# Two graph layers on one core: where the operands of the second layer lie, and what TensorE does ahead of the last transposes of the first

## The chip, the cores and the metric

The kernel runs on one core of a Trainium2 chip. The metric is the device time of one execution in microseconds (us); the time of the kernel before is the median of 3 runs. Beside it there is one profiled execution with a trace of every engine. TensorE is PE in the profile (PEld is its load of weights), VectorE is DVE, ScalarE is ACT, GpSimd is POOL, and SyncE (SP) issues most of the DMAs.

## The reference

x is 2500 x 1024, there are 80,000 edges with a source, a destination (sorted, and denser at low numbers) and a weight. Cut to what matters:

```python
h = relu(layernorm(x))
x = x + segment_sum((h @ W0)[src] * edge_weight[:, None], dst)      # layer 1
h = relu(layernorm(x))
row, col = dst plus every node itself as destination, src plus every node itself as source
deg = number of edges in each row (the node itself counted)
dis = deg ** -0.5
x = x + segment_sum((dis[row] * dis[col])[:, None] * (h @ W1.T + b)[col], row)   # layer 2
```

In the second layer no edge has a weight of its own. So its sum is a product of a matrix of counts (2500 x 2500, how many edges run from one node to another, the node itself included) with the rows dis * (h @ W1.T + b), and dis once more on the outside.

## The kernel before

The nodes lie in 20 tiles of 128 rows (the last has 68). Layer 1 first makes `support` = h @ W0 for all tiles (L281). Then each tile of destinations is summed: the four thickest tiles (0 to 3) as products with dense weight matrices (`multiplied`, L588), the other 16 by gathers of 128 rows of `support` at a time (`gathered`, L564): POOL gathers a block into `msg` (8 buffers), DVE makes a one-hot matrix, ACT makes `hi` and DVE `lo`, two parts of the weighted rows for matmuls in a faster format, and PE adds four matmuls of them to `sums` (L581). When a tile's sums are complete, `finish` (L540) adds x (L543), normalizes (`normed`, DVE and ACT), transposes (`transposed`, L530: 8 transposes on PE, copied by ACT), multiplies with W1 (L554, 16 matmuls in plain fp32, two halves of 512 columns), adds the bias (L558) and stores the result in `hid_d[t]`. Along with this, `count_group` builds the matrix of counts tile by tile, `counts`, which is stored as `cnat` (L497) and summed into `total`.

Layer 2 begins at L667: `deg` is the sum over `total`, `dis` follows from it (L668 to L670). Then comes the flag `missing` (L671 to L681): it tells whether any edge found no place, by a matmul with ones (L676) and comparisons of its result; at the very end of the program a second, general way is taken if it is not zero. After `first.close()` (L682) the pools of layer 2 are opened. For every tile, in the order of `ORDER`, a row buffer (3 of them) is loaded from `hid_d[t]` (L691), ACT makes `hi` (L693) and DVE `lo` (L695): both stay in SBUF for the whole of layer 2, 8 KB in each partition for a tile. For each row of tiles `counts_of` loads the counts with a transposing DMA into `cT` (L701, two buffers) and ACT casts them to `bT` (L703, two buffers). 80 matmuls (L721: 20 tiles, hi and lo, two halves) make the sums of one row; rows 0 and 1 are made together, so that each operand tile serves 8 matmuls as soon as it is there. `row` (L706) adds x1 and stores.

What sets the order: every engine runs its own list of instructions in the order that a scheduler fixed when the program was built. The scheduler takes an instruction when its own estimate says that it is ready, and of those that are ready the one that stands first in the code; so work that stands late in the code can run early. `order_behind(i, other)` (L273) tells it that `i` must come after `other` on the same engine. The tiles and the counting of layer 1 are dealt out by a plan written by hand (L464 to L663).

What sets the places: SBUF pools are laid one after the other from the low end, those with `side="right"` from the high end, and a closed pool's bytes are given out again. With `reuse_waits="tile"` a tile waits only for the users of the bytes that it covers; without it, for all users of the pools beneath. The sizes in one partition, from the code: `keep` 2 KB, then `lay` (total, bias, src_p, row_p, wgt_p, base_i, low, key, wpart, iota16, in this order) about 30 KB, `work` 25, `ohs` 15.5, `cpool` 15.4, `wpool` (the 8 pieces of W1) 32.8, `dense` (4 matrices of 10.2) 41; from the right `gather` (msg 8 x 4.1, oh_r, hi, lo) 50.7. Layer 2 has `lay2` (20 tiles x 8.2 KB), which begins where `lay` began, and then `work2` (rows 3 x 4.1, cT 2 x 5.1, bT 2 x 10.2), 43 KB. [...]Before, one pool holds pT (2 banks), mm (2 x 2), cb (2), in the order of their first use; `psum2` of layer 2 lays three sums `mm2` of 2 banks each over the first six.

Of the kernel before, what the change touches and what calls it, by code (L numbers as in the profile page):

```python
# [9 lines left out]
F32 = mybir.dt.float32  # L10
F32R = mybir.dt.float32r
# [5 lines left out]
ALU = mybir.AluOpType  # L17
DVE = mybir.EngineType.DVE

P = 128  # L20
# [18 lines left out]

OPENING = 8  # L40
TAIL = 48

ORDER = (3, 4, 5, 6, 2, 7, 8, 9, 1, 10, 11, 12, 13, 0, 14, 15, 16, 17, 18, 19)

# [2 lines left out]
def direct(  # L47
# [26 lines left out]
    nc = tc.nc  # L74
# [14 lines left out]
    def rows(t):  # L89
        return min(P, N - t * P)  # L90
# [24 lines left out]


    first = ctx.enter_context(ExitStack())
    lay = first.enter_context(tc.tile_pool(name="lay", bufs=1))
    work = first.enter_context(tc.tile_pool(name="work", bufs=2))
    psum = first.enter_context(tc.tile_pool(name="psum", bufs=2, space=bass.MemoryType.PSUM))  # L120
    ohs = first.enter_context(tc.tile_pool(name="ohs", bufs=8))
    cpool = first.enter_context(tc.tile_pool(name="cpool", bufs=3))
    wpool = first.enter_context(tc.tile_pool(name="wpool", bufs=1, reuse_waits="tile"))
    sup_ctx = tc.tile_pool(name="sup", bufs=4, side="right")
    sup = sup_ctx.__enter__()
    prep_ctx = tc.tile_pool(name="prep", bufs=1)
# [158 lines left out]

    def products(t):
        hT, rstd = ready.pop(t)
        mm = psum.tile([P, 2, H], F32, name="mm")
        yield from product(hT, w0_sb, mm)
        row = sup.tile([P, D], F32, name="row", bufs=2)  # L290
        nc.scalar.activation(row, mm.rearrange("p h d -> p (h d)"), AF.Copy, scale=rstd)
        nc.sync.dma_start(support[t * P:t * P + rows(t), :], row[:rows(t), :])
# [123 lines left out]
    def count_group(t, g, a, b):  # L416
        nonlocal last_count

        w = WINDOWS[t][1]
        if t not in counts:  # L420
            counts[t] = cpool.tile([P, NT, P], F16, name="counts")
            nc.scalar.copy(counts[t].rearrange("p t w -> p (t w)"), zero.to_broadcast([P, NT * P]))
            nc.vector.tensor_copy(counts[t][:, t, :rows(t)], ident[:, :rows(t)])
            if t < DENSE:
                dense[t] = dpool.tile([P, NT, P], F32, name="dense")
                nc.scalar.copy(dense[t].rearrange("p t w -> p (t w)"), zero.to_broadcast([P, NT * P]))
        if g % 4 == 0:
            bases[t] = nc.values_load_multi_w_load_instructions(
                base_i[0:1, g:g + 4], engines=[DVE], min_val=0, max_val=P - w,
                skip_runtime_bounds_check_because="a row of a tile")[1]  # L430
        v = bases[t][g % 4]
        cb = psum.tile([P, 512], F32, name="cb")
        ab = []
        for k in range(a, b):
            oh_low = ohs.tile([P, P], BF, name="oh_low")
            nc.vector.tensor_scalar(oh_low, iota16[:, :P], low[:, k:k + 1], None, op0=ALU.is_equal)  # L436
            oh_key = ohs.tile([P, KW], BF, name="oh_key")
            nc.vector.tensor_scalar(oh_key[:, :NT * w], iota16[:, :NT * w], key[:, k:k + 1], None,  # L438
                                    op0=ALU.is_equal)
            last_count = nc.tensor.matmul(  # L440
                cb[:, :NT * w], oh_low, oh_key[:, :NT * w], start=(k == a), stop=(k == b - 1))
            if t < DENSE:
                wl = ohs.tile([P, 3, P], BF, name="wl")
                for i in range(3):
                    nc.scalar.activation(wl[:, i, :], oh_low, AF.Copy, scale=wpart[:, i, k:k + 1])  # L445
                ab.append((wl, oh_key))
        to = counts[t][:, :, ds(v, w)]
        nc.vector.tensor_tensor(to, cb[:, :NT * w].rearrange("p (t w) -> p t w", w=w), to, op=ALU.add)  # L448
        if t < DENSE:
            for j, (wl, oh_key) in enumerate(ab):  # L450
                for i in range(3):
                    last_count = nc.tensor.matmul(  # L452
                        cb[:, 256:256 + NT * w], wl[:, i, :], oh_key[:, :NT * w],
                                     start=(j == 0 and i == 0), stop=(j == len(ab) - 1 and i == 2))
            to = dense[t][:, :, ds(v, w)]
            nc.vector.tensor_tensor(to, cb[:, 256:256 + NT * w].rearrange("p (t w) -> p t w", w=w), to,
                                    op=ALU.add)
        if b == K0[t + 1]:
            nc.vector.tensor_tensor(total, counts[t], total, op=ALU.add)
            to_store.append([6, t])  # L460
# [66 lines left out]
    gpool = first.enter_context(tc.tile_pool(name="gather", bufs=2, side="right", reuse_waits="tile"))  # L527


    def transposed(v, into):  # L530
        for k0 in range(0, KC, 4):
            pT = psum.tile([P, 4, P], F32, name="pT")
            for k in range(4):
                nc.tensor.transpose(pT[:, k, :], v[:, (k0 + k) * P:(k0 + k + 1) * P], ident)  # L534
            nc.scalar.copy(into[:, k0:k0 + 4, :], pT)
            yield 0.7, 0.0, 0.6

# [85 lines left out]

    def steps_of(tiles):
        for t in tiles:
            sums = psum.tile([P, 2, H], F32, name="mm")
            n = NT if t < DENSE else TILE_BLOCKS[t]
            for j, took in enumerate((multiplied if t < DENSE else gathered)(t, sums)):
                if j == n - 1:
                    rest = finish(t, sums)  # L630
                    takes(*next(rest))
                    waiting.append(rest)
                yield took
# [34 lines left out]
    nc.vector.tensor_scalar(dis, deg, 1.0, None, op0=ALU.max)  # L668
    nc.scalar.activation(dis, dis, AF.Sqrt)
    nc.vector.reciprocal(dis, dis)  # L670
    nc.vector.tensor_reduce(placed[:, 1:2], deg, axis=mybir.AxisListType.X, op=ALU.add)  # L671
    over = lay.tile([P, NT], F32, name="over")
    nc.vector.tensor_scalar(over, deg, 2048.0, None, op0=ALU.is_gt)
    nc.vector.tensor_reduce(placed[:, 2:3], over, axis=mybir.AxisListType.X, op=ALU.add)
    ps = psum.tile([P, 4, P], F32, name="pT")
    nc.tensor.matmul(ps[:, 0, :3], ones, placed, start=True, stop=True)  # L676
    lost = lay.tile([1, 3], F32, name="lost")
    for i, n in enumerate((E, E + N, 0)):
        nc.vector.tensor_scalar(lost[:, i:i + 1], ps[0:1, 0, i:i + 1], float(n), None, op0=ALU.not_equal)
    nc.vector.tensor_add(lost[:, 0:1], lost[:, 0:1], lost[:, 1:2])  # L680
    nc.vector.tensor_add(missing, lost[:, 0:1], lost[:, 2:3])  # L681
    first.close()  # L682


    lay = ctx.enter_context(tc.tile_pool(name="lay2", bufs=1, reuse_waits="tile"))
    work = ctx.enter_context(tc.tile_pool(name="work2", bufs=2, reuse_waits="tile"))
    psum = ctx.enter_context(tc.tile_pool(name="psum2", bufs=2, space=bass.MemoryType.PSUM, reuse_waits="tile"))
    his, los = {}, {}
    for t in ORDER:
        hf = work.tile([P, D], F32, name="rows", bufs=3)  # L690
        nc.sync.dma_start(hf, hid_d[t])  # L691
        his[t] = lay.tile([P, D], F32R, name=f"hi{t}")
        nc.scalar.activation(his[t], hf, AF.Copy, scale=dis[:, t:t + 1])  # L693
        los[t] = lay.tile([P, D], F32R, name=f"lo{t}")
        nc.vector.scalar_tensor_tensor(los[t], hf, dis[:, t:t + 1], his[t].bitcast(F32),  # L695
                                       op0=ALU.mult, op1=ALU.subtract)

# [8 lines left out]
    def row(r, mm):  # L706
        xh = work.tile([P, D], F32, name="rows", bufs=3)
        nc.sync.dma_start(xh, x1_d[r])
        nc.vector.scalar_tensor_tensor(xh, mm.rearrange("p h d -> p (h d)"), dis[:, r:r + 1], xh,  # L709
                                       op0=ALU.mult, op1=ALU.add)  # L710
        nc.sync.dma_start(out[r * P:r * P + rows(r), :], xh[:rows(r), :])


    for rs in [(0, 1)] + [(r,) for r in range(2, NT)]:
        bTs = [counts_of(r) for r in rs]
        mms = [psum.tile([P, 2, H], F32, name="mm2", bufs=3) for r in rs]
        for k in ORDER:
            for bT, mm in zip(bTs, mms):
                for v in (his[k], los[k]):
                    for h in range(2):  # L720
                        nc.tensor.matmul(mm[:, h, :], bT[:rows(k), k, :], v[:rows(k), h * H:(h + 1) * H],  # L721
                                         start=(k == ORDER[0] and v is his[k]),
                                         stop=(k == ORDER[-1] and v is los[k]))
        for r, mm in zip(rs, mms):
            row(r, mm)


def kernel(tc, edges, xT, *args):
# [338 lines left out]
```

## Time and profile before

| what | us |
|---|---|
| median of 3 runs (1786.69 to 1789.98) | 1788.44 |
| the profiled execution | 1799.45 |
| its span, first to last instruction | 1797.5 |
| counting ends: last store of counts (L497) | 1124.4 |
| last dense matmul (L594) | 1286.1 |
| last `lo` of the gathers (L577) begins | 1385.5 |
| sums of the last tile added to x (L543) begin | 1390.1 |
| last tile's transposes (L534) begin | 1396.7 |
| first matmul of layer 2 (L721) begins | 1413.1 |
| rows 0 and 1 done, first output step (L709) begins | 1457.5 |
| last output step (L709) begins | 1789.0 |

A timeline line reads: start, duration, engine, line, operation, output <- inputs, shapes, count, and in brackets how long the engine was idle before it and what ended that. A line of the chain of work that ended last reads: start, duration, engine, output, line. In a table of windows each engine has its busy time and its number of instructions.

### The profile page before, as it was taken

How to read it: one execution, taken by the hardware profiler on the slowest of the kernel's cores; microseconds unless marked ns; L12 is line 12 of the kernel's file. 1: busy time of each engine (PE TensorE's matmuls, PEld its weight loads, DVE VectorE, ACT ScalarE, POOL GpSimd, SP SyncE). 2: the span in 40 equal slices, each digit the busy share in tenths (PEclk: the TensorE clock that was granted, in tenths of full speed). 3: DMA queues.
4: the chain of work that ended last, by engine and by line, in shares of the span. 5: the costliest groups of instructions: out<-in, count | busy, mean ns of one | idle time of the engine just before them, and what ended most of it. 6: DMA issues, size and time to landing. Idle time of an engine off the chain costs nothing. (4 is left out here: it accounts for less than half of the span.)

```text
span 1797.5 us, 21334 instructions
## 1 busy us (share of the span) xinstructions
PE 1674.1 (93%) x6506; PEld 1036.6 (58%) x6506; DVE 1207.7 (67%) x3051; ACT 903.0 (50%) x1476; POOL 479.4 (27%) x457
## 2 busy tenths in 40 slices
PE   6999999999788897988999998999899999999998
PEld 2465555544354554544556554655566568888886
DVE  5788888898698796888899897877787330000000
ACT  3499999961165454455456443555565431111110
POOL 3000000000066453555545544555463000000000
PEclk9999999999899998999999999999999999999999
DMA  8413121132799896898889888988986874342420
GB/s 274 171 37 97 51 77 60 39 83 71 242 350 355 281 314 235 281 342 259 300 307 329 307 268 278 344 321 320 320 298 212 229 196 108 77 115 76 115 62 32
DMA packets 217329, 369.95 MB, mean 206 GB/s; under 512 B 115662, under 2 KB 135128, under 8 KB 217206
## 3 DMA queue, kind: packets, MB, share of 16 engines
q0 software_dynamic: 54832, 199.25, 31.5%
q1 hardware_dynamic: 162374, 169.25, 30.0%
q8 instruction: 53, 0.87, 0.2%
q14 instruction: 70, 0.57, 0.1%
HBM read 300.79 MB, written 54.56 MB: 198 GB/s over the span
## 5 line engine op out<-in xcount | busy, mean ns | idle before, releaser
L575 ACT ACTIVATE hi<-msg,wgt_p 128x1024 fp32r<-128x1024 f32 x378 | 426.1, 1147 | 375.9 <-PE mm L581 281.1
L569 POOL DMA_INDIRECT msg<-support,src_p x378 | 464.1, 1228 | 515.2 <-DVE lo L577 178.0
L577 DVE SCALAR_TENSOR_TENSOR lo<-msg,wgt_p,hi 128x1024 fp32r<-128x1024 f32 x378 | 478.7, 1281 | 94.9 <-ACT hi L575 54.2
L281 PE MATMUL mm<-w,hT 128*128 128x512 f32 x640 | 314.4, 603 | 2.4 <-ACT hT L173 2.4
L581 PE MATMUL mm<-hi,oh_r 128*128 128x512 f32 x756 | 291.0, 466 | 19.9 <-ACT hi L575 14.6
L554 PE MATMUL pT<-w,vT 128*128 128x512 f32 x640 | 303.1, 595 | 0.0
L581 PE MATMUL mm<-lo,oh_r 128*128 128x512 f32 x756 | 280.4, 451 | 16.9 <-DVE lo L577 16.0
L445 ACT ACTIVATE wl<-oh_low,wpart 128x128 bf16<-128x128 bf16 x891 | 262.0, 418 | 0.0
L721 PE MATMUL mm<-lo,bT 128*128 128x512 f32 (+1 forms) x800 | 248.1, 392 | 3.7 <-DVE lo L695 3.3
L721 PE MATMUL mm<-hi,bT 128*128 128x512 f32 (+1 forms) x800 | 247.6, 392 | 3.3 <-ACT bT L703 2.0
L709 DVE SCALAR_TENSOR_TENSOR rows<-mm,dis,rows 128x1024 f32<-128x1024 f32 x20 | 25.7, 1284 | 308.0 <-PE mm L721 307.3
L594 PE MATMUL mm<-msg,dense 128*128 128x512 f32 (+1 forms) x320 | 166.6, 636 | 38.9 <-DMA msg<-support 38.9
L581 PEld LDWEIGHTS mm<-hi,oh_r 128*128 128x128 f32 x756 | 141.7, 192 | 103.2 <-issue 46.4
L581 PEld LDWEIGHTS mm<-lo,oh_r 128*128 128x128 f32 x756 | 138.3, 192 | 102.8 <-DVE lo L577 49.5
L438 DVE TENSOR_SCALAR oh_key<-iota,key 128x200 bf16<-128x200 f16 (+12 forms) x675 | 195.5, 292 | 3.0 <-PE cb L452 2.8
L703 ACT CAST bT<-cT 128x2560 fp32r<-128x2560 f16 x20 | 46.6, 2335 | 261.3 <-PE mm L721 257.8
L554 PEld LDWEIGHTS pT<-w,vT 128*128 128x128 f32 x640 | 120.8, 190 | 94.5 <-issue 80.4
L721 PEld LDWEIGHTS mm<-lo,bT 128*128 128x128 f32 (+1 forms) x800 | 149.8, 188 | 40.0 <-DVE lo L695 8.9
L721 PEld LDWEIGHTS mm<-hi,bT 128*128 128x128 f32 (+1 forms) x800 | 150.3, 189 | 36.3 <-ACT bT L703 2.4
L448 DVE TENSOR_TENSOR counts<-cb,counts 128x200 f32 (+13 forms) x296 | 138.9, 470 | 47.6 <-PE cb L440 40.8
L436 DVE TENSOR_SCALAR oh_low<-iota,low 128x128 bf16<-128x128 f16 x675 | 168.3, 253 | 1.3 <-ACT wl L445 1.1
L281 PEld LDWEIGHTS mm<-w,hT 128*128 128x128 f32 x640 | 107.8, 192 | 62.9 <-issue 56.7
(141 smaller groups left out, 1144.4 us busy)
## 6 DMA issues: line engine op xcount, KB each, us to landing
msg<-support SPq DMA_DIRECT2D x76, 512.0 KB
xt<-in_x SPq DMA_DIRECT2D x38, 512.0 KB
cnat<-counts SPq DMA_DIRECT2D x20, 640.0 KB
x_d<-xt SPq DMA_DIRECT2D x20, 512.0 KB
hid_d<-hn SPq DMA_DIRECT2D x20, 512.0 KB
rows<-hid_d SPq DMA_DIRECT2D x20, 512.0 KB
rows<-x_d SPq DMA_DIRECT2D x20, 512.0 KB
hT<-in_xT SPq DMA_DIRECT2D x19, 512.0 KB
```

Of the source, the lines that this page charges most:

```text
L281: on_pe(nc.tensor.matmul(mm[:, h, :], vT[:, k, :], ws[k][:, h * H:(h + 1) * H], start=(k == 0), stop=(k == KC - 1)))
L436: nc.vector.tensor_scalar(oh_low, iota16[:, :P], low[:, k:k + 1], None, op0=ALU.is_equal)
L438: nc.vector.tensor_scalar(oh_key[:, :NT * w], iota16[:, :NT * w], key[:, k:k + 1], None, op0=ALU.is_equal)
L445: nc.scalar.activation(wl[:, i, :], oh_low, AF.Copy, scale=wpart[:, i, k:k + 1])
L448: nc.vector.tensor_tensor(to, cb[:, :NT * w].rearrange("p (t w) -> p t w", w=w), to, op=ALU.add)
L554: on_pe(nc.tensor.matmul(mm, vT[:, k, :], w1_sb[k][:, h * H:(h + 1) * H], start=(k == 0), stop=(k == KC - 1)))
L569: nc.gpsimd.indirect_dma_start(out=msg, out_offset=None, in_=support, in_offset=bass.IndirectOffsetOnAxis(ap=src_p[:, k:k + 1], axis=0))
L575: nc.scalar.activation(hi, msg, AF.Copy, scale=wgt_p[:, k:k + 1])
L577: nc.vector.scalar_tensor_tensor(lo, msg, wgt_p[:, k:k + 1], hi.bitcast(F32), op0=ALU.mult, op1=ALU.subtract)
L581: i = nc.tensor.matmul(sums[:, h, :], oh, v[:, h * H:(h + 1) * H], start=(j == 0 and v is hi), stop=(j == n - 1 and v is lo))
L594: i = nc.tensor.matmul(sums[:, h, :], dense[t][:rows(k), k, :], msg[:rows(k), h * H:(h + 1) * H], start=(k == 0), stop=(k == NT - 1))
L721: nc.tensor.matmul(mm[:, h, :], bT[:rows(k), k, :], v[:rows(k), h * H:(h + 1) * H], start=(k == ORDER[0] and v is his[k]), stop=(k == ORDE ...
```

## The change

The pools of layer 1 are laid in another order, and PSUM is split into three pools (cb, mm, pT). Layer 2's operands are in two pools: `late` for the last 11 tiles of ORDER, laid in reverse order from where `lay` began, then `work2`, then `early` for the first 9 tiles. The loads and splits stand inside the loop over the tiles of rows 0 and 1. The first of the last tile's 8 transposes (`turned[-KC]`) is put behind the 24th matmul of layer 2. The flag is computed after row 4, with a buffer of mm2 for its matmul.

```diff
+EARLY = 9
+BETWEEN = 3
...
-    lay = first.enter_context(tc.tile_pool(name="lay", bufs=1))
-    work = first.enter_context(tc.tile_pool(name="work", bufs=2))
+    lay = first.enter_context(tc.tile_pool(name="lay", bufs=1, reuse_waits="tile"))
+    work = first.enter_context(tc.tile_pool(name="work", bufs=2, reuse_waits="tile"))
+    psum_c = first.enter_context(tc.tile_pool(name="psum_c", bufs=2, space=bass.MemoryType.PSUM))
+    psum_m = first.enter_context(tc.tile_pool(name="psum_m", bufs=2, space=bass.MemoryType.PSUM))
     psum = first.enter_context(tc.tile_pool(name="psum", bufs=2, space=bass.MemoryType.PSUM))
-    ohs = first.enter_context(tc.tile_pool(name="ohs", bufs=8))
-    cpool = first.enter_context(tc.tile_pool(name="cpool", bufs=3))
     wpool = first.enter_context(tc.tile_pool(name="wpool", bufs=1, reuse_waits="tile"))
+    ohs = first.enter_context(tc.tile_pool(name="ohs", bufs=8, reuse_waits="tile"))
+    cpool = first.enter_context(tc.tile_pool(name="cpool", bufs=3, reuse_waits="tile"))
...
-        mm = psum.tile([P, 2, H], F32, name="mm")
+        mm = psum_m.tile([P, 2, H], F32, name="mm")
...
-        cb = psum.tile([P, 512], F32, name="cb")
+        cb = psum_c.tile([P, 512], F32, name="cb")
...
+    turned = []
+
     def transposed(v, into):
...
-                nc.tensor.transpose(pT[:, k, :], v[:, (k0 + k) * P:(k0 + k + 1) * P], ident)
+                turned.append(nc.tensor.transpose(pT[:, k, :], v[:, (k0 + k) * P:(k0 + k + 1) * P], ident))
...
-            sums = psum.tile([P, 2, H], F32, name="mm")
+            sums = psum_m.tile([P, 2, H], F32, name="mm")
...
-    nc.vector.tensor_reduce(placed[:, 1:2], deg, axis=mybir.AxisListType.X, op=ALU.add)
-    over = lay.tile([P, NT], F32, name="over")
...
-    nc.vector.tensor_add(missing, lost[:, 0:1], lost[:, 2:3])
     first.close()
-    lay = ctx.enter_context(tc.tile_pool(name="lay2", bufs=1, reuse_waits="tile"))
+    psum = ctx.enter_context(tc.tile_pool(name="psum2", bufs=2, space=bass.MemoryType.PSUM, reuse_waits="tile"))
+    late = ctx.enter_context(tc.tile_pool(name="late", bufs=1, reuse_waits="tile"))
+    his, los = {}, {}
+
+    def parts_of(t, pool):
+        his[t] = pool.tile([P, D], F32R, name=f"hi{t}")
+        los[t] = pool.tile([P, D], F32R, name=f"lo{t}")
+
+    for t in ORDER[:EARLY - 1:-1]:
+        parts_of(t, late)
     work = ctx.enter_context(tc.tile_pool(name="work2", bufs=2, reuse_waits="tile"))
-    psum = ctx.enter_context(tc.tile_pool(name="psum2", bufs=2, space=bass.MemoryType.PSUM, reuse_waits="tile"))
-    his, los = {}, {}
-    for t in ORDER:
+    early = ctx.enter_context(tc.tile_pool(name="early", bufs=1, reuse_waits="tile"))
+    for t in ORDER[:EARLY]:
+        parts_of(t, early)
+
+    def split(t):
         hf = work.tile([P, D], F32, name="rows", bufs=3)
         nc.sync.dma_start(hf, hid_d[t])
-        his[t] = lay.tile([P, D], F32R, name=f"hi{t}")
         nc.scalar.activation(his[t], hf, AF.Copy, scale=dis[:, t:t + 1])
-        los[t] = lay.tile([P, D], F32R, name=f"lo{t}")
         nc.vector.scalar_tensor_tensor(los[t], hf, dis[:, t:t + 1], his[t].bitcast(F32),
                                        op0=ALU.mult, op1=ALU.subtract)
...
+    def all_placed():
+        nc.vector.tensor_reduce(placed[:, 1:2], deg, axis=mybir.AxisListType.X, op=ALU.add)
+        over = keep.tile([P, NT], F32, name="over")
+        nc.vector.tensor_scalar(over, deg, 2048.0, None, op0=ALU.is_gt)
+        nc.vector.tensor_reduce(placed[:, 2:3], over, axis=mybir.AxisListType.X, op=ALU.add)
+        ps = psum.tile([P, 2, H], F32, name="mm2", bufs=3)
+        nc.tensor.matmul(ps[:, 0, :3], ones, placed, start=True, stop=True)
+        lost = keep.tile([1, 3], F32, name="lost")
+        for i, n in enumerate((E, E + N, 0)):
+            nc.vector.tensor_scalar(lost[:, i:i + 1], ps[0:1, 0, i:i + 1], float(n), None, op0=ALU.not_equal)
+        nc.vector.tensor_add(lost[:, 0:1], lost[:, 0:1], lost[:, 1:2])
+        nc.vector.tensor_add(missing, lost[:, 0:1], lost[:, 2:3])
...
     for rs in [(0, 1)] + [(r,) for r in range(2, NT)]:
         bTs = [counts_of(r) for r in rs]
         mms = [psum.tile([P, 2, H], F32, name="mm2", bufs=3) for r in rs]
         for k in ORDER:
+            if rs[0] == 0:
+                split(k)
             for bT, mm in zip(bTs, mms):
                 for v in (his[k], los[k]):
                     for h in range(2):
-                        nc.tensor.matmul(mm[:, h, :], bT[:rows(k), k, :], v[:rows(k), h * H:(h + 1) * H],
+                        i = nc.tensor.matmul(mm[:, h, :], bT[:rows(k), k, :], v[:rows(k), h * H:(h + 1) * H],
...
+            if rs[0] == 0 and k == ORDER[BETWEEN - 1]:
+                order_behind(turned[-KC], i)
         for r, mm in zip(rs, mms):
             row(r, mm)
+        if rs[0] == 4:
+            all_placed()
```

More of the change, by code (lines that the diff above doesn't have):

```diff
@@ L670, in direct @@
     nc.vector.reciprocal(dis, dis)
-    nc.vector.tensor_reduce(placed[:, 1:2], deg, axis=mybir.AxisListType.X, op=ALU.add)
-    over = lay.tile([P, NT], F32, name="over")
[L673 to L680, printed above, removed]
-    nc.vector.tensor_add(missing, lost[:, 0:1], lost[:, 2:3])
-    first.close()
-    lay = ctx.enter_context(tc.tile_pool(name="lay2", bufs=1, reuse_waits="tile"))
+    first.close()
+    psum = ctx.enter_context(tc.tile_pool(name="psum2", bufs=2, space=bass.MemoryType.PSUM, reuse_waits="tile"))
[6 more added lines that the diff above has]
+        parts_of(t, late)
     work = ctx.enter_context(tc.tile_pool(name="work2", bufs=2, reuse_waits="tile"))
-    psum = ctx.enter_context(tc.tile_pool(name="psum2", bufs=2, space=bass.MemoryType.PSUM, reuse_waits="tile"))
-    his, los = {}, {}
-    for t in ORDER:
+    early = ctx.enter_context(tc.tile_pool(name="early", bufs=1, reuse_waits="tile"))
+    for t in ORDER[:EARLY]:
+        parts_of(t, early)
+    def split(t):
         hf = work.tile([P, D], F32, name="rows", bufs=3)
         nc.sync.dma_start(hf, hid_d[t])
-        his[t] = lay.tile([P, D], F32R, name=f"hi{t}")
         nc.scalar.activation(his[t], hf, AF.Copy, scale=dis[:, t:t + 1])
-        los[t] = lay.tile([P, D], F32R, name=f"lo{t}")
         nc.vector.scalar_tensor_tensor(los[t], hf, dis[:, t:t + 1], his[t].bitcast(F32),
@@ L720, in direct @@
                     for h in range(2):
-                        nc.tensor.matmul(mm[:, h, :], bT[:rows(k), k, :], v[:rows(k), h * H:(h + 1) * H],
-                                         start=(k == ORDER[0] and v is his[k]),
-                                         stop=(k == ORDER[-1] and v is los[k]))
+                        i = nc.tensor.matmul(mm[:, h, :], bT[:rows(k), k, :], v[:rows(k), h * H:(h + 1) * H],
+                                             start=(k == ORDER[0] and v is his[k]),
+                                             stop=(k == ORDER[-1] and v is los[k]))
+            if rs[0] == 0 and k == ORDER[BETWEEN - 1]:
+                order_behind(turned[-KC], i)
         for r, mm in zip(rs, mms):
             row(r, mm)
+        if rs[0] == 4:
+            all_placed()
 def kernel(tc, edges, xT, *args):
```

## The prediction

> **What bounds the kernel now.** I read the page first, then the window table round the change from layer 1 to layer 2, then the timeline, the waits and the chain there. TensorE (PE) is the engine with the most work:
>
> ```profile
> span 1797.5 us, 21334 instructions
> PE 1674.1 (93%) x6506; PEld 1036.6 (58%) x6506; DVE 1207.7 (67%) x3051; ACT 903.0 (50%) x1476; POOL 479.4 (27%) x457
> ```
>
> so a gain has to come from a place where PE stands still. The window table (PE, PEld, DVE, ACT, POOL, clock, DMA share, GB/s) shows where that is:
>
> ```profile
> 1390.00:1400.00 10.00, 9.65 (x30) 4.58 (x29) 3.74 (x7) 2.71 (x4) 0.00 (x0) 1.00 0.86 236
> 1400.00:1410.00 10.00, 10.00 (x25) 4.46 (x24) 0.69 (x1) 5.70 (x3) 0.00 (x0) 1.00 0.91 207
> 1410.00:1420.00 10.00, 8.57 (x33) 5.60 (x31) 5.41 (x10) 3.34 (x3) 0.00 (x0) 1.00 0.68 224
> 1420.00:1440.00 20.00, 17.92 (x71) 12.71 (x71) 11.90 (x10) 10.36 (x9) 0.00 (x0) 1.00 0.72 222
> 1440.00:1460.00 20.00, 16.57 (x66) 11.28 (x65) 11.03 (x10) 10.51 (x9) 0.00 (x0) 1.00 0.77 232
> 1460.00:1480.00 20.00, 20.00 (x81) 16.36 (x82) 0.81 (x1) 2.11 (x1) 0.00 (x0) 0.91 0.72 173
> ```
>
> Up to 1410 PE is full (L554, the last two products of layer 1). From 1410 to 1460 it is not, though it has only the L721 matmuls to do; from 1460 it is full to the end. The timeline names what it stood for:
>
> ```profile
> 1396.74 0.60 PE L534 MATMUL pT<-ident,hn 128*128 128x128 f32 x4
> 1398.17 13.90 PE L554 MATMUL pT<-w,vT 128*128 128x512 f32 x32
> 1411.91 0.28 PE L676 MATMUL pT<-placed,ones 128*128 128x3 f32 x2
> 1413.13 0.93 PE L721 MATMUL mm<-hi,bT 128*128 128x512 f32 x3 [0.94 <-DVE lost L680]
> 1414.56 0.73 PE L721 MATMUL mm<-lo,bT 128*128 128x512 f32 x2 [0.49 <-DVE lo L695]
> ```
>
> First the flag: the first sums of layer 2 lie in the PSUM banks of pT, whose last reader is the flag (L676 to L680). Then the operands hi and lo. Why these come late is in the timeline of ACT, and how they go on in the chain:
>
> ```profile
> 1412.84 2.19 ACT L693 ACTIVATE hi<-rows,dis 128x1024 fp32r<-128x1024 f32 x2 [4.68 <-DVE hn L558]
> ...
> 1418.15 1.16 ACT hi L693
> 1419.34 1.29 DVE lo L695
> 1420.65 3.25 DMA rows<-hid_d
> ...
> 1454.88 2.60 PE mm L721 x10
> 1457.56 2.33 ACT bT L703
> 1459.94 329.03 PE mm L721 x1440
> ```
>
> The pool of hi and lo begins where pool lay began: lo3 and hi4 lie over the bias, which L558 reads until 1412.8. ACT stands for that, with dis ready since 1140. After that the loop of three row buffers (load, hi, lo, load again) turns once in some 6.4 us, one operand tile in 2.14 us ((1453.5 - 1419.3) / 16), while PE needs 8 matmuls of 329.03 / 1440 = 0.2285 us, 1.83 us, for it. So the bound of this stretch is the supply of hi and lo, and it started too late.
>
> [...] busy time alone reads 10.00 of 10 with the starts 0.43 us apart (L554); so I count starts and gaps between them. [...] the second hi stood 4.68 us, and nothing ran on ACT in it. So an instruction that is put in early and isn't ready blocks all behind it. [...] with gathers running the windows show a DMA share of 0.79 to 0.99, so loads that move there meet them.
>
> **The change part by part.** I take the profiled execution, 1799.45 us with a span of 1797.5; the median is 1788.44, 11.0 us less. The stretch that changes is the same piece of work in both, so I take the difference in us over to the median.
>
> *The sums' banks and the flag.* Removed: PE's step from the end of L554 to the first L721, 1411.91 to 1413.13, 1.22 us. With psum_c and psum_m ahead of psum, the first sums lie over cb (last used 1117.6) and the second over an mm buffer (free after L543 at 1391.3 at the latest). Moved: the flag's matmul (two loads and two short matmuls, 0.43 us apart at 1411.5 and 1411.9) goes into PE's stream at row 4. It costs 0.2 to 0.9 there; I take 0.45. Its third sums buffer isn't missed, as a row takes 80 x 0.2285 = 18.3 us; its seven or eight small DVE steps (about 1.1 us) lie in DVE's 93% idle time of layer 2. Net gain 0.8.
>
> *The places of hi and lo.* By the sizes in the code, the 9 tiles of pool early begin some 15 KB into dense: those of tiles 3, 4 and 5 lie in it (last read at 1286.1, for some of them by tile 1 far earlier), the next six over the gather pool (last read by L577 at 1386.8, L581 at 1389.4). The 11 of pool late lie over lay, work and w. So before the last product ends six more tiles can be made: three from rows loaded ahead (1.3 us each at DVE's rate), three after one more turn of the loop (6.4): done by about 1387 + 3.9 + 6.4 + 2.6 = 1400. The last product ends at 1396.9 + 5.5 (the 24 matmuls) + 1.4 (transposes) + 13.7 = 1417.5. PE then has six tiles in hand, 11 us. Tile 10 lies over w6 and w7 and starts at 1417.6; its lo is done at 1420. Tiles 11 and 12 follow at 1.3 us, and from there the loop gives one in 2.14: the last at some 1441. PE asks for the last at 1417.5 + 16 x 1.83 = 1446.8. The loop never becomes the bound again, with 5 us to spare. Removed: the 160 matmuls of rows 0 and 1 took 1413.13 to 1457.48, 44.35 us; at 0.2285 they take 36.56. Gain **7.8**.
>
> *The 24 matmuls ahead of the transposes.* They are the same matmuls, so no PE time is added. They hide the last tile's norm: sums ready 1390.0, hn at 1394.85; L554 of tile 18 hides this now until 1396.7, with 1.9 us to spare, and with hi and lo of six tiles put between on ACT and DVE that would not last. With 5.5 us more, cover is 7.4. The transposes themselves wait for a pT copy both before and after (1.43 us): gain 0 to 0.4, and up to 1.2 lost if a 1.15 us hi stands in front of each copy; I take 0. The new wait has behind it on PE the last tile's transposes, its whole product and the rest of layer 2: if bT or hi is late, all of that is late by the same.
>
> *What is moved without being named.* The scheduler doesn't keep the order of the code: deg and dis (L667 to L670) ran at 1124.9 to 1139.7, 270 us ahead of their neighbours. So the loads of cT and three rows, the two casts bT (2.33 each), and hi and lo of tiles 3 to 5 can go to ACT, DVE and SP as soon as counts are stored (1124.4) and dense is free, in among the gathers. On ACT that is 2 x 2.33 + 3 x 1.15 = 8.1 us, on DVE 3 x 1.28 = 3.8, side by side. Between 1120 and 1390 hi has two buffers, and PE was kept by hi or lo for 10.2 + 11.5 + 4.8 us in all, so part of it reaches PE. Bounds 0 and 8.1. As ACT is half idle there (10 to 12 of 20), I take 1.0. DMA: in layer 2 a row's cT and two 0.5 MB transfers take a share of about 0.36 of 18.3 us, 6.6 us; less 2.8 for the two at 375 GB/s leaves 3.8 for a cT. Two to four cT and three rows are 12 to 20 us of DMA among gathers that are issued 12 to 19 us ahead of use: hidden by that lead if spread out. On SP a cT holds the queue for up to 5.2 us, with msg<-support, xt, x_d and hid_d behind it; they have 8 buffers of lead, so I take nothing, bounds 0 and 5.
>
> *What stays.* bT of row 2 has two buffers, so 1457.56 to 1459.94 stays (2.4 us), as does all after it.
>
> Sum: 0.8 + 7.8 + 0 - 1.0 = **7.6 us**. Profiled 1799.45 - 7.6 = 1791.85; median 1788.44 - 7.6 = **1780.8** (-0.42%). About 0.2%, 3.6 us, is what a measurement here can tell from no change.
>
> **The rivals.**
> 1. *Moved work hurts the gathers more, gain used up.* Cost 5 to 12 in place of 1: 1784.9 to 1791.9, within 0.2%. For it: DVE has up to 19.9 of 20 us busy near 1130 and 1330, DMA share 0.98. Against: POOL stood for free buffers, 54.7 us for DVE's lo alone; gathers are limited by buffers and not by DMA.
> 2. *Slower.* One mechanism: a cast bT stands in ACT's queue in the gather stage before its cT has landed. In this trace the first cT took from 1393.11 to 1400.50, 7.4 us. Two casts at 7.4 + 2.33 block ACT for 19.5 us; the two hi buffers cover one block, 2.7 us, each time: 14 lost, net 14 - 8.6 = +5.5: **1794**. It decides from a lost time of 12.2 us. Against: ACT is given a cast when the planner thinks the load done, so only its error counts.
> 3. *It doesn't do what it says*: hi and lo are made no earlier, since SP's row loads stay behind other waits (SP stood 10.0 us for a gather buffer at 1376.7). Then only the flag's 0.8 and perhaps one turn of the loop: 1786, within 0.2%.
> 4. *More*: with free operands the matmuls fill real gaps of PE in the gather stage (11 us idle from 1100 to 1400); up to 5.5 more, less what the norm then shows: 1776.
>
> **How the numbers follow.** As worked out 0.60 (own range 1778.5 to 1784.5), rival 1 0.14, rival 2 0.09, rival 3 0.07, rival 4 0.10. The range 1775.5 to 1788 takes in the first case, rivals 3 and 4 and the nearer half of rival 1. Faster: 0.60 + 0.10 + 0.06 from the edges of rivals 1 and 3; same 0.15; slower 0.09.
>
> **What would show it.** Right: 24 L721 ahead of the last L534; the row of the chain from the last L554 straight to L721; no wait of L721 for lo or hi; the span from the last product's end to the bT of row 2 near 31 us (136 matmuls); L676's successor at row 4. Wrong: a PE wait for bT before the transposes, ACT hi L575 waiting for a bT, or PE idle between 1120 and 1390 grown by more than 3 us.

## The result and the profile after

| | median, us | ratio to before, 95% interval |
|---|---|---|
| before (6 runs beside the changed kernel) | 1786.36 | |
| changed (6 runs, 1801.45 to 1809.11) | 1804.45 | 1.0091 [1.0071, 1.0111] |

Some 16 us slower by the ratio (18.1 by these two medians), where 7.6 us faster was predicted. The profiled execution of the changed kernel took 1804.6 us (span 1802.7). The kernel before, profiled once more on another chip, had a span of 1786.5, close to its median, and the same order of instructions as in the first profile; I compare with that second profile where sums are made. The time of both is cut at three points that both have: the last dense matmul of layer 1 begins, the last-but-one product with W1 begins (the 16 matmuls of 7.03 us), row 2 of layer 2 begins.

| stage, us | before, first profile | before, second | changed | changed less second |
|---|---|---|---|---|
| up to the last dense matmul | 1284.81 | 1275.72 | 1277.11 | +1.39 |
| gathers | 105.06 | 103.54 | 128.27 | **+24.73** |
| from layer 1 to row 2 of layer 2 | 70.07 | 69.84 | 59.82 | **-10.02** |
| row 2 to the end | 337.56 | 337.40 | 337.50 | +0.10 |
| span | 1797.5 | 1786.5 | 1802.7 | +16.2 |

Each column is one execution. The 1.39 us of the first row are within what two profiles of the same kernel differ by (9.1 us in that row); the 24.73 us are far outside it (1.5 us in theirs).

So two things happened. The stage that the prediction worked out gave even more than its 8.6 us. The stage ahead of it, for which the prediction set down a loss of 1.0 us, lost 24.7.

**The part that came as predicted.** The changed kernel's timeline of PE round the turn to layer 2 (start, duration, engine, line, operation, shapes, count, idle time before and what ended it):

```profile
1405.38 7.03 PE L563 MATMUL pT<-w,vT 128*128 128x512 f32 x16
1411.85 1.03 PE L745 MATMUL mm<-hi,bT 128*128 128x512 f32 x2
...
1417.74 1.04 PE L543 MATMUL pT<-ident,hn 128*128 128x128 f32 x8
1418.54 0.48 PE L745 MATMUL mm<-hi,bT 128*128 128x512 f32 x1
1419.02 14.00 PE L563 MATMUL pT<-w,vT 128*128 128x512 f32 x32
1432.46 0.79 PE L745 MATMUL mm<-hi,bT 128*128 128x512 f32 x1
...
1465.20 0.73 PE L745 MATMUL mm<-hi,bT 128*128 128x512 f32 x2 [1.51 <-ACT bT L711]
```

24 matmuls of layer 2 (L745) stand ahead of the transposes (L543), and between 1405 and 1463 no line has a bracket: PE waits neither for the flag nor for hi or lo. The wait for row 2's bT has stayed.

**The part that didn't.** The windows from 1280 to 1320 (PE, PEld, DVE, ACT, POOL with busy time and count; TensorE's clock; DMA share; GB/s), first before (second profile, whose last dense matmul begins 1.4 us earlier than in the changed kernel), then changed:

```profile
1280.00:1300.00 20.00, 18.00 (x58) 11.17 (x59) 16.30 (x28) 12.30 (x15) 10.90 (x12) 0.91 0.99 385
1300.00:1320.00 20.00, 20.00 (x75) 12.81 (x73) 17.72 (x23) 14.04 (x14) 13.46 (x11) 1.00 0.87 311
```

```profile
1280.00:1300.00 20.00, 14.82 (x46) 9.08 (x46) 12.81 (x22) 7.45 (x9) 8.02 (x7) 0.91 1.19 185
1300.00:1320.00 20.00, 3.03 (x5) 1.81 (x6) 3.26 (x7) 8.62 (x7) 1.50 (x1) 0.60 1.04 293
```

From 1300 to 1320 PE worked 3 of 20 us, and so did DVE; POOL issued one gather. In the 20 us ahead of that the DMA engines were busier than before (share 1.19 against 0.99) and moved half as much (185 GB/s against 385). The timeline of ACT tells who held the stage:

```profile
1291.18 1.15 ACT L584 ACTIVATE hi<-msg,wgt_p 128x1024 fp32r<-128x1024 f32 x1
1304.77 2.32 ACT L711 CAST bT<-cT 128x2560 fp32r<-128x2560 f16 x1 [12.43 <-DMA cT<-cnat]
1307.00 0.29 ACT L147 ACTIVATE rstd<-mv,eps 128x1 f32<-128x1 f32 x1
1313.54 2.33 ACT L711 CAST bT<-cT 128x2560 fp32r<-128x2560 f16 x1 [6.25 <-DMA cT<-cnat]
1315.77 2.19 ACT L584 ACTIVATE hi<-msg,wgt_p 128x1024 fp32r<-128x1024 f32 x2
```

The two casts of rows 0 and 1 stand among the gathers' hi (L584). ACT stood 18.7 us for the loads of counts and made no hi from 1292.3 to 1315.8; PE then waited for hi:

```profile
1316.97 1.22 PE L590 MATMUL mm<-hi,oh_r 128*128 128x512 f32 x2 [17.97 <-ACT hi L584]
```

The timeline of SP shows the loads, which came behind the gathers before (there the longest issue was 5.2 us):

```profile
1282.04 9.73 SPq L709 DMA_TRANSPOSE cT<-cnat  x1
1291.87 0.52 SPq L553 DMA_DIRECT2D x_d<-xt  x1
1292.44 18.95 SPq L709 DMA_TRANSPOSE cT<-cnat  x1
```

Two things are thus wrong at once: the casts wait on ACT (theory A), and the transposing loads take the DMA engines from the gathers (theory B). Which of them makes the loss isn't to be read from one trace. A third theory (C) was that the loss has nothing to do with these moves.

### The profile page after: what moved, and what is told of

Same layout as the page of the kernel before. It is cut to its first block, busy times and chain, and to the rows that moved or that the text cites. A ratio compares the mean times of both kernels' runs of the same rounds, so it can differ in the third digit from the quotient of the medians.

```text
span 1802.7 us, 21316 instructions
## 1 busy us (share of the span) xinstructions
PE 1668.4 (93%) x6506; PEld 1037.0 (58%) x6506; DVE 1206.6 (67%) x3051; ACT 902.7 (50%) x1476; POOL 474.0 (26%) x457
## 5 line engine op out<-in xcount | busy, mean ns | idle before, releaser
L584 ACT ACTIVATE hi<-msg,wgt_p 128x1024 fp32r<-128x1024 f32 x378 | 426.6, 1147 | 372.4 <-PE mm L590 277.8
L578 POOL DMA_INDIRECT msg<-support,src_p x378 | 458.7, 1213 | 536.0 <-DVE lo L586 199.9
L586 DVE SCALAR_TENSOR_TENSOR lo<-msg,wgt_p,hi 128x1024 fp32r<-128x1024 f32 x378 | 478.4, 1280 | 98.8 <-ACT hi L584 69.6
L745 PE MATMUL mm<-hi,bT 128*128 128x512 f32 (+1 forms) x800 | 248.1, 391 | 1.5 <-ACT bT L711 1.5
L745 PE MATMUL mm<-lo,bT 128*128 128x512 f32 (+1 forms) x800 | 246.6, 389 | 0.0
L590 PEld LDWEIGHTS mm<-lo,oh_r 128*128 128x128 f32 x756 | 138.5, 193 | 103.6 <-DVE lo L586 53.0
L745 PEld LDWEIGHTS mm<-hi,bT 128*128 128x128 f32 (+1 forms) x800 | 150.1, 188 | 33.8 <-ACT bT L711 1.9
L745 PEld LDWEIGHTS mm<-lo,bT 128*128 128x128 f32 (+1 forms) x800 | 150.2, 188 | 31.8 <-issue 0.2
```

Source lines behind the costliest of these rows:

```text
L578: nc.gpsimd.indirect_dma_start(out=msg, out_offset=None, in_=support, in_offset=bass.IndirectOffsetOnAxis(ap=src_p[:, k:k + 1], axis=0))
L584: nc.scalar.activation(hi, msg, AF.Copy, scale=wgt_p[:, k:k + 1])
L586: nc.vector.scalar_tensor_tensor(lo, msg, wgt_p[:, k:k + 1], hi.bitcast(F32), op0=ALU.mult, op1=ALU.subtract)
L590: i = nc.tensor.matmul(sums[:, h, :], oh, v[:, h * H:(h + 1) * H], start=(j == 0 and v is hi), stop=(j == n - 1 and v is lo))
L745: i = nc.tensor.matmul(mm[:, h, :], bT[:rows(k), k, :], v[:rows(k), h * H:(h + 1) * H], start=(k == ORDER[0] and v is his[k]), stop=(k == ...
```

## The experiments

The kernel before once more, unchanged:

> The kernel before, unchanged, profiled once more on another chip. The profiled execution shown first took 1799.45 us, 13 us over the later median of 1786.36; from 1116 to 1390 us it and the changed kernel run the same orders up to about 1280, so a second profile tells how long the gathers take when undisturbed. Expected by all theories: 1783 to 1800, with the piece from the last 16 matmuls of tile 18's product to the first matmul of row 2 at 70 us as before.

1788.35 us, span 1786.5. It gave the second column of the table above: the first profile's extra 11 us lie ahead of the last dense matmul (9.1) and in the gathers (1.5), not in the stage that the prediction is about.

The first three edits were measured against 49 runs of the kernel before with a median of 1789.98. They hold back the loads, the casts, or both, in the changed kernel:

```diff
# loads held
+        if r < 2:
+            order_behind(i, gathers[-1])        # i: the transposing load of cT
# casts held
+        if r < 2:
+            order_behind(i, his_of_blocks[-1])  # i: the cast bT <- cT
```

> The changed kernel, with the two transposing loads of rows 0 and 1 put behind the last gather on the list of orders. Theory A (in ACT's queue the casts of rows 0 and 1 stand before the gathers' hi and wait for loads that are slow amid gathers): the 18 us wait of TensorE goes, and what the change was to bring remains, 1775 to 1780, 8 to 10 us under before. Theory B (the two loads themselves take so much DMA time from the gathers that these come late): the same, 1775 to 1780. Theory C (the loss lies elsewhere in the change: early row loads, the place of the pools): 1798 to 1806.

> The changed kernel, with the loads left where they are, amid the gathers, and only the two casts on ACT put behind the last hi of the gathers. Theory A: nothing waits for the loads in the gather stage, so 1775 to 1781. Theory B: the gathers are still robbed of DMA time for some 20 us a load, TensorE still stands for 8 to 18 us, 1785 to 1798. Theory C: 1798 to 1806.

> The changed kernel with loads behind the last gather and casts behind the last hi of the gathers. Theories A and B: 1774 to 1779, the least of these, since in the run with loads alone held a cast may still wait a little for a load. Theory C: 1798 to 1806. If this is slower than the run with loads alone held, the casts come too late for the 24 matmuls ahead of the transposes.

| kernel | median, us | ratio [interval] | gathers, us | to row 2, us |
|---|---|---|---|---|
| loads held | 1792.86 | 1.0023 [1.0008, 1.0038] | 118.99 | 59.78 |
| casts held | 1804.84 | 1.0079 [1.0054, 1.0105] | 133.63 | 59.96 |
| both held | 1781.24 | 0.9953 [0.9936, 0.9970] | 105.99 | 60.76 |

The medians are of all runs, the stages of one profiled execution each. Loads and gathers are issued by different engines, and the order binds them only in the program's plan: with the loads held, the first went out at 1356.0, 1.1 us ahead of the last gather, in place of 1282.0.

With both held the predicted gain is there: 8.4 us by the ratio, where 7.6 was predicted. C falls. But neither edit is enough alone, which no theory had foreseen: the loads held came between the ranges of A and B and that of C, the casts held above B's 1785 to 1798. Both held came 2 us above the range of A and B. With the casts held, ACT is free, and the stage is still the longest of all; the waits between 1270 and 1390 of that kernel (who waited for whom: us in total, times, longest) have moved from the casts to the gathers themselves:

```profile
ACT hi L585 <- DMA msg<-support,src_p: 29.5, 5, 15.1
```

PE stood for these hi 6.7 and 14.2 us. So B costs the whole loss without A. With the loads held, the casts still stand ahead of the last hi, and the cast waits at a later place. That kernel's timeline of ACT:

```profile
1375.39 2.32 ACT L714 CAST bT<-cT 128x2560 fp32r<-128x2560 f16 x1 [15.05 <-DMA cT<-cnat]
```

PE waited 12.4 us behind it. So A costs too where the load is slow: its cT was issued at 1356.0 and came 19.4 us later, with the last gather issued at 1357.1. That makes the load's slowness the question. What does it share with the gathers?

**What of the load is slow.** Three kernels replace the transposing load of rows 0 to 3 by an ordinary one of the same bytes; they leave out the transposition of these rows' counts. They differ in the size of the pieces and in whether the casts are held:

```diff
-        nc.sync.dma_start_transpose(out=cT..., in_=cnat[r]...)
+        if r < 4:   # 5 KB per partition
+            nc.sync.dma_start(cT.rearrange("p t s -> p (t s)"), cnat[r].rearrange("t p d -> (t p d)").rearrange("(p f) -> p f", p=P))
# or, 256-byte pieces:
+            nc.sync.dma_start(cT, cnat[r].rearrange("t p d -> p t d"))
```

The first ran against 55 runs of the kernel before with a median of 1789.85, the other two against 40 with 1789.69.

> The changed kernel with the casts of rows 0 and 1 held behind the last hi of the gathers, the loads of their counts left among the gathers, and the counts of rows 0 to 3 loaded by an ordinary transfer of 5 KB per partition in place of the transposing one. It leaves out the transposition of these four rows' counts; bytes, instructions and the work after them are the same. If it is the transposing transfer that robs the gathers, the loads land in some 3 us each, TensorE is full again from 1280 to 1360 and the time is near that of the kernel with both held: 1779 to 1785. If any load of 0.65 MB at this place robs them, the time stays near that of the casts held alone: 1800 to 1806. With SP's queue alone as the cause (the issue holds SP for 10 to 27 us, which an ordinary issue doesn't), it would also be near 1781; the length of the issues and the share of the DMA engines then tell these two apart.

> The changed kernel with one edit: the counts of rows 0 to 3 come by an ordinary transfer with 5 KB per partition. It leaves out the transposition of these four rows' counts. The order of the instructions on every engine stays that of the changed kernel, and nothing is held; the two casts stand in ACT's queue in the gather stage as before. Theory: the slow transposing transfer is the one root, and the casts waited (18.7 us) only because it was slow: 1778 to 1784, ratio 0.993 to 0.997, and the cast's wait shrinks below 5 us. Rival: the place of the casts costs by itself: with the loads quick the time still is near that of the loads held alone, ratio 1.000 to 1.003.

> The changed kernel with the casts of rows 0 and 1 held, and the counts of rows 0 to 3 among the gathers by an ordinary transfer in pieces of 256 bytes, 2560 to a load, about as small as the pieces that the trace shows for the transposing one (10904 packets under 512 bytes for four). It leaves out the transposition of these four rows' counts. If it is the small packets that rob the gathers: near the transposing loads, 1.006 to 1.010. If it is what the transposing transfer does beyond being cut small: near the 5 KB pieces, 0.993 to 0.998.

| kernel | median, us | ratio [interval] | gathers, us | to row 2, us |
|---|---|---|---|---|
| 5 KB pieces, casts held | 1777.91 | 0.9939 [0.9922, 0.9956] | 106.19 | 59.81 |
| 5 KB pieces, nothing held | 1783.90 | 0.9970 [0.9956, 0.9983] | 106.43 | 59.81 |
| 256-byte pieces, casts held | 1775.47 | 0.9924 [0.9899, 0.9948] | 103.92 | 59.81 |

With the casts held only the loads of rows 0 and 1 lie among the gathers, as cT has two buffers; with nothing held all four do. Expected from the transposing transfer as the root were 1779 to 1785, 1778 to 1784 and 0.993 to 0.998; the first and third came a little faster. The second row is the cleanest: every engine's instructions stand in the order of the changed kernel, with the casts and the loads among the gathers, and only the kind of the transfer differs. The ratio falls from 1.0091 to 0.9970, the gathers from 128.27 to 106.43 us (in the fastest of its 22 runs, 1777.62), and the casts waited 1.8 us instead of 18.7. So it is the transposing that costs: 21.8 of the 24.7 us in these traces, and enough to turn the loss into a gain. It isn't the small pieces: with 256-byte pieces and the casts held the gathers took 103.92 us, with the transposing load and the casts held 133.63. That SP's queue is held by long issues is no likely cause either: with 256-byte pieces SP was held 12.90 us by the three loads of rows and 5.81 us by a store, and PE was busy 20.00 of 20 us from 1300 to 1320. The DMA view of ten microseconds shows it directly (packets and what they moved; then for each queue packets, MB and the time that its packets took as a share of 16 engines; queue 0 has the gathers, queue 1 SP's transfers; then the issues, with the median us to landing). First the changed kernel from 1286 to 1296, then the one with 5 KB pieces and nothing held from 1280 to 1290:

```profile
DMA packets 1968, 0.92 MB, mean 92 GB/s; under 512 B 1860, under 2 KB 1860, under 8 KB 1967
q1 hardware_dynamic: 1884, 0.61, 112.8%
q0 software_dynamic: 83, 0.30, 14.4%
msg<-support,src_p POOLq DMA_INDIRECT x5, 19.4
```

```profile
DMA packets 1044, 4.11 MB, mean 411 GB/s; under 512 B 104, under 2 KB 104, under 8 KB 1043
q1 hardware_dynamic: 592, 2.44, 60.7%
q0 software_dynamic: 451, 1.66, 41.4%
```

With the transposing load in flight the engines were busy all the time and moved 0.92 MB instead of 4.11, the gathers 0.30 instead of 1.66. The five gathers took 19.4 us to land, where the seven that were issued from 1270 to 1280, ahead of the loads, took 7.4. It wasn't so all along. From 1307 to 1311, shortly before the second load landed, the gathers moved 1.20 MB (300 GB/s) and only the load was slow, with 0.12 MB (30 GB/s); from 1311 to 1313 no gather was left in flight, and the load moved 0.57 MB (285 GB/s). Why the gathers had their rate back there, no run shows. The kernel with the loads held shows both cases of the transposing load one after the other: with gathers still landing (1366 to 1376), and with none (1376 to 1386):

```profile
q1 hardware_dynamic: 2891, 0.73, 103.6%
q0 software_dynamic: 104, 0.37, 22.6%
```

```profile
q1 hardware_dynamic: 5604, 1.91, 81.1%
```

0.73 MB in 1.036 x 10 us is 70 GB/s; once queue 0 is empty, 1.91 MB in 8.1 us is 235 GB/s (a store of 0.5 MB is in that, too). By the same count, the load that was alone from 1311 to 1313 in the changed kernel had 0.57 MB in 1.289 x 2 us, 221 GB/s. With gathers at 22.6% of the engines' time the load ran at a third of that. What remains open is whether any second queue does this or the gathers alone: no kernel put ordinary transfers of another queue in their place. Open, too, is why holding the casts gave 0.9939 against 0.9970 with plain loads, 5.5 us by the ratios; so a cost of the casts' place itself, without a slow load, isn't ruled out. The profiled executions of the two don't show it (106.19 and 106.43, 59.81 both), but that of the second was 6.3 us under its median.

**The other parts of the change.** The order for the 24 matmuls, taken out of the kernel with both held, and the flag with the PSUM pools alone, put into the kernel before (against 55 runs of before with a median of 1789.85):

```diff
# without the 24
-            if rs[0] == 0 and k == ORDER[BETWEEN - 1]:
-                order_behind(turned[-KC], i)
# flag alone, on the kernel before
+    psum_c = ...    # cb
+    psum_m = ...    # mm
+        if rs[0] == 4:
+            all_placed()
```

> The kernel with loads and casts both held, without the order that puts 24 matmuls of layer 2 ahead of the last tile's transposes (the planner then puts 4 ahead). My prediction's term for the 24: between -1.2 and +0.4 us of gain, taken as 0; cover for the norm falls from 7.4 to about 3 us. Theory: 0 to +2 us against the kernel with the order, ratio to the kernel before 0.9953 to 0.9965. Rival: the norm's wait is uncovered since hi and lo of six tiles stand ahead of it on ACT and DVE: +3 us or more, 0.997 or above.

> The kernel before with two parts of the change alone: the PSUM pool split in three, and the flag computed after row 4. Pools of SBUF, loads, casts and the 24 matmuls are as before. Prediction's term: 0.8 us of gain, 0 to 1.2, ratio 0.9993 to 1.0000. Rival: in the kernel before, hi and lo of the first tiles end no earlier than the flag, so the wait of 0.94 us passes to lo and nothing is gained: ratio 1.0000 within its interval; then the first matmul of layer 2 waits for hi or lo in place of the flag.

Without the 24: 1780.31 us, 0.9950 [0.9930, 0.9970], the same as with them within the intervals; the way to row 2 took 61.54 us against 60.76, so they are worth 0.8 us in the one trace of each. The rival's 3 us of uncovered norm didn't come.

Flag alone: 1790.44 us, 1.0002 [0.9981, 1.0022], and 69.54 us to row 2 against 69.84. The interval doesn't tell 0.8 us from nothing. The timeline of PE shows the rival's wait:

```profile
1400.93 1.26 PE L727 MATMUL mm<-hi,bT 128*128 128x512 f32 x3
1403.66 0.72 PE L727 MATMUL mm<-lo,bT 128*128 128x512 f32 x2 [1.46 <-DVE lo L686]
```

Layer 2 now begins straight after the last product and three matmuls later waits for lo. The wait for the flag stood beside a wait for operands; alone its removal gains 0.3 us in the trace.

**Two tries for more**, on the kernel with both held. Row 0's matmuls over the last four tiles before row 1's, so that row 2's cast runs beside row 1; and on top of that the first three loads of rows behind the last gather:

```diff
# row 0 first
+        steps = [(k, bT, mm) for k in ORDER if k not in last for bT, mm in zip(bTs, mms)]
+        steps += [(k, bT, mm) for bT, mm in zip(bTs, mms) for k in last]
# rows held
+        if t in ORDER[:3]:
+            order_behind(i, gathers[-1])   # i: the load of rows
```

> The kernel with loads and casts both held, and over the last four tiles all matmuls of row 0 before those of row 1, so that row 0's buffer of counts is free 7.3 us before row 1 ends and row 2's cast runs beside row 1. Theory: the gap of TensorE at row 2 (1.5 to 2.4 us) goes, and with it the 3.4 us at half clock that follow it (worth up to 1.7 us): 1.5 to 4 us less than with both held, 1777 to 1780, ratio 0.993 to 0.9945. Rival: row 2's transposing load lands late, or the cast meets row 0's own end on ACT, and the gap stays: no difference.

> The kernel with both held and row 0 first over the last four tiles, and the three first loads of layer 1's stored rows held behind the last gather as well. Theory: these three loads of 0.5 MB meet the gathers at 1281 to 1288 and cost some of the 3.5 us by which the stage of the gathers was later than in the kernel before: 0 to 3 us of gain, ratio 0.992 to 0.994. Rival: they are hidden by the gathers' lead, as ordinary loads of the counts were: no difference within 0.2%, and holding them can cost 1 to 3 us if hi and lo then come late for the 24 matmuls.

Row 0 first: 1774.26 us, 0.9941 [0.9915, 0.9966]. Its way to row 2 took 58.74 us against 60.76, and row 2 begins without a bracket, 0.46 us behind the matmul group before. The gap is gone; the medians' interval is too wide to tell its 2 us from the kernel with both held. It has the lowest median of the kernels that compute everything, and is faster than both the kernel before and the changed one.

Rows held: 1783.73 us, 0.9967 [0.9949, 0.9984]; the gathers took 105.03 us against 103.98 in one execution each, so nothing shows that these loads had been in the gathers' way. The rival's price came instead, in PE's timeline:

```profile
1396.48 0.50 PE L757 MATMUL mm<-hi,bT 128*128 128x512 f32 x1 [2.16 <-ACT hi L705]
1399.99 2.93 PE L564 MATMUL pT<-w,vT 128*128 128x512 f32 x3 [3.00 <-ACT vT L544]
```

hi comes late, and behind it on ACT the copy of the transposes.

## Why the prediction was wrong

*The banks and the flag, 0.8.* The step from the last product to layer 2, 1.22 us before, is gone in the changed kernel. The flag's matmul at row 4 costs 0.23 us of PE: around it two matmuls start 0.37 and 0.31 us after the one before instead of 0.23. Gained 1.0; but it takes both parts of the change, since alone the wait passes to lo (0.3). That the rest took the same time (337.50 against 337.40) is luck: the changed kernel has no stretch at half clock behind row 2's start, so that it came to its last matmul 1.4 us sooner (327.23 against 328.61), and from there to the end it took 1.4 us longer (10.24 against 8.85; the other kernels lie between 8.9 and 10.2).

*The places of hi and lo, 7.8.* Right. From the first matmul of layer 2 to row 2, the 24 ahead of the transposes included, 46.81 us (first profile; 46.58 in the second) became 5.89 + 0.48 + 32.74 = 39.11: 7.7 or 7.5, with 0.5 of it from the shorter wait for row 2. The supply of lo never became the bound again.

*The 24 matmuls, 0 (bounds -1.2 to +0.4).* Too low, without weight: leaving them out cost 0.8 us in the trace, and from the last-but-one product to the end of the last, these 24 not counted, the changed kernel took 20.71 us against 22.04 in the second profile. These 1.3, with 1.2 and 7.5 from the two terms above, are the 10.0 us of this stage.

*What stays, 2.4.* Most of it stayed: PE shows 1.51 us of idle time ahead of row 2, and 2.02 before.

*What is moved without being named, 1.0.* This is the step that failed. The prediction named what moves (two to four cT, three loads of rows, two casts), the place (among the gathers, once dense is free) and the queues. It was wrong in the price of the transposing load. It took 3.8 us of DMA for one, an estimate from layer 2, where no gather runs (with 375 GB/s for the two transfers beside it, the rate that the trace of before has from 1200 to 1220 and from 1240 to 1260), and let the gathers' lead hide all of it, "12 to 20 us of DMA among gathers that are issued 12 to 19 us ahead of use: hidden by that lead if spread out". Among gathers a load took 21.0 us to land (the second; the first was still waited for 22.7 us after its issue; 4.8 is the median of the run), the two held SP 9.7 and 19.0 us, and the gathers beside them landed after 19.4 us instead of 7.4, which used up their lead. Its bounds, 0 to 8.1 for ACT and 0 to 5 for SP, were made of busy times of instructions and of the share of the DMA engines; none allowed for a transfer that changes the speed of others. The measured cost is 24.7 us. PE's idle times of over 0.3 us in the stage grew from 2.8 us (second profile) to 24.3: one of the prediction's own signs of being wrong, set at 3 us.

*Rival 2* had the place and the mechanism of what the trace shows: a cast at the head of ACT's queue before its cT has landed. It gave 19.5 us of blocked ACT, 14 lost and 1794; ACT was kept from hi for 23.4 us and PE stood 17.97 us for it, so the buffers covered 5.4 us, the two times 2.7 of the rival's sum. It had the load's slowness too small (7.4 us, taken from a stage without gathers), and it was a part of the cause: with the casts out of the way hi waited for the gathers themselves, and the time stayed. Against it stood that the planner (the scheduler that fixes the order) places a cast when it thinks the load done, so only its error counts; that error was 12.4 and 6.3 us.

The sum of the two traces: 10.0 gained on the way to layer 2, 24.7 lost among the gathers, 1.4 before them and 0.1 after: 16.2 us slower.

## What to carry to other kernels

When a change of places in memory frees an operand's bytes earlier, its load moves too, whether the edit names it or not: list what becomes ready and look at what runs there. A transfer's price was not a number of its own here but depended on what was in flight beside it (4.8 or 21 us to landing), so take it from a stage with the same neighbours, and if there is none, give the cost no upper bound and put that into the range. And the consumer of a load that is moved early blocks the queue it stands in until the load has landed (18.7 us on ACT); holding it back was not enough here, as the load itself was in the gathers' way.

## What the runs showed of the hardware

A transposing load of 0.65 MB and a stream of indirect gathers slowed each other far beyond sharing for most of the time that both were in flight: by the time of its packets the load ran at 70 GB/s with the loads held (1366 to 1376), where the one that was alone in the changed kernel (1311 to 1313) had 221, and the changed kernel's gathers landed after 19.4 us instead of 7.4. At its worst the total was 92 GB/s where an ordinary load beside the same gathers had 411. Near the end of the second load only the load was slow (30 GB/s beside gathers at 300, then 285 without them). Pieces of 256 bytes in an ordinary load don't do it (365 GB/s from 1283 to 1303). By the lines above, a packet of the load's queue took 57 ns on average beside gathers (103.6% of 16 engines' 10 us over 2891 packets) and 23 ns without them (81.1% over 5604).

After idle times of 1.5 to 3 us TensorE ran at about half clock in some of the traces. Eleven of the thirteen have 1.51 to 2.02 us of idle time ahead of row 2. In four of these (both of before, both held, 256-byte pieces) matmuls then came at 0.43 us instead of 0.23 for some 3.4 us: in the first profile of before, after 2.02 us, 8 matmuls took from 1460.97 to 1464.34; with both held, after 1.51 us, 8 took from 1443.54 to 1446.90. In the other seven they came at 0.23 us, in the changed kernel after 1.51 us and with the flag alone after 2.01 us among them. With the rows held, the clock from 1400 to 1405 was 0.59 behind the idle time of 3.00 us. What decides it no run shows.
